# Bias seeds as four matmul passes on 32-row tiles, the three parts of the bias side by side in each row group

## The chip, the cores and the metric

The kernel runs on one core of a Trainium2 chip. The metric is the device time of one execution in microseconds (us), the median of the runs. Times inside an execution come from one profiled execution and count from the start of its span.

## The reference

Two layers, each with a residual and a layer norm, on x of 32 batches of 512 x 1024 f32. Layer 0 is a graph attention; layer 1 multiplies by W = adj * adj and adds a bias. It is this bias that the change is about.

```python
# layer 0: q, k = wq.x, wk.x over the 512 channels; scores = leaky_relu(q + k)
att = softmax(scores, axis=-1)
agg = einsum('bcn,bmn->bcm', x, att)
x = layernorm(x + relu(einsum('oc,bcm->bom', adj, agg) + bm[None, :, None]))
# layer 1
W = adj * adj
x = layernorm(x + einsum('bnf,nm->bmf', x, W) + bias)    # bias has 1024 elements
```

## The kernel before, in words

The work goes batch by batch, with four batches in flight. For each batch the kernel projects x (`project`, L320, into PSUM banks A, B and C), ranks the 1024 query values instead of forming the 1024 x 1024 softmax (`place` L390, `count` L417), scatters the projected rows by rank into a table in DRAM (`send` L403), reads the table back in blocks (`fetch` L445), forms prefix sums with nine small matmul steps (`table` L494, `table_out` L506, `carry` L515, `table_store` L521), gathers each row's sums from the table (`pick` L532), mixes them (`scale`, `gain`), turns the result (`turn` L584), adds the residual and normalises (`add`, `square`, `root0`, `finish` L614, which writes the four tiles of y at L619 on ScalarE), and then multiplies by W with a seven-product scheme (`multiply` L660) into PSUM banks A, B and C. `read` (L675) takes the products out, and `stats`, `root`, `shift`, `apply` and `store` finish the batch.

The order of all steps is written out by hand, as lists of step names: `BEGIN` (L844) for the start-up, `SLOT` (L910) once for each turn of the loop, 28 turns in all, and `END` (L874). Each engine takes its instructions in that order; SP issues the loads, table transfers and stores in that order too, and GpSimd (POOL) issues the indirect DMAs.

The bias enters through PSUM. `seed_bias` (steps sb0, sb1, sb2 in `BEGIN`) splits the f32 bias, broadcast over 128 partitions in y[:, 0], into three bf16 parts, one after the other: VectorE casts what is left of the bias into the bf16 view of y[:, 1] (L203, 128 x 1024), copies one row of it into `seeds` (L205), and subtracts the part from the bias (L209). Part i goes into partition 32 * i of a 128-row tile that is zero elsewhere. The first half of the 1024 columns is the bias of the left half, the second half the difference of right and left (L202). `seed` (L645, steps sA and sB) then begins the accumulation in banks A and B of each batch with two passes each: a matmul of an all-ones 128 x 128 stationary with the 128 x 512 rows of `seeds`, so that every output row receives the sum of the three parts. In `SLOT` the order on TensorE is t8 (table step, L501), sA, sB, then m0, m1, m3, m2, m6 and so on (L666); m6 is the first product that needs the last two tiles of y. In `BEGIN` sB and sA of batch 0 are apart, and in `END` the pairs are in part apart.

In `BEGIN` the steps around the bias are, in order: sb0, a few projections, fe (the fetch of batch 0), sb1, sb2, and then c0 (`count`, L419, on ScalarE). For the first two batches `count` and `place` write their unneeded output into y[:, 1] (`junk`, L277), which is the buffer that also holds the bf16 part of the bias.

Of the kernel before, what the change touches and what calls it, by code (L numbers as in the profile page):

```python
# [9 lines left out]
BF16 = mybir.dt.bfloat16  # L10
# [13 lines left out]
def gat_gcn_resnorm_kernel(  # L24
# [11 lines left out]
    nc = tc.nc  # L36
    P = 128
# [3 lines left out]
    H = 512  # L41
# [13 lines left out]
    const = ctx.enter_context(tc.tile_pool(name="const", bufs=1))  # L55
# [19 lines left out]
    for i, a in enumerate((wq, wk, bm)):  # L75
        nc.scalar.dma_start(
            out=vec[i * CT : (i + 1) * CT, :], in_=a.rearrange("(t p) -> t p", p=P)
        )
    nbm = const.tile([P, CT], F32, name="nbm")
    seeds = const.tile([P, 2, H], BF16, name="seeds")  # L80
    nc.vector.memset(seeds, 0.0)
    ones = const.tile([P, 1], BF16, name="ones")
    nc.vector.memset(ones, 1.0)
# [3 lines left out]
    for half in range(2):  # L87
        p0 = half * G
        nc.gpsimd.affine_select(
            out=tri[p0 : p0 + G, 0, :], in_=tri[p0 : p0 + G, 0, :], pattern=[[-2, G]],  # L90
# [3 lines left out]
            out=tri[p0 : p0 + G, 1, :], in_=tri[p0 : p0 + G, 1, :], pattern=[[2, G]],  # L94
# [3 lines left out]
    for row, i in ((0, 0), (G, 1)):  # L98
# [14 lines left out]
        out=first, in_=first, pattern=[[-1, 2 * N - P]], compare_op=ALU.is_ge,  # L113
# [28 lines left out]
    for td in tdb:  # L142
        nc.sync.dma_start(
            out=td.rearrange("(s u) c -> s u c", u=3)[N:NS, 0, :], in_=zs[P + N - NS : P, 0, 0:ZW]
        )
        odd = td.rearrange("(s w u) c -> s w (u c)", w=2, u=3)
        for r in range(0, NS // 2, P):
            n = min(P, NS // 2 - r)
            nc.sync.dma_start(
                out=odd[r : r + n, 0, ZW : 3 * ZW].rearrange("p (j c) -> p j c", j=2)[:, :, 0:1],  # L150
                in_=zs[0:n, 0:2, 1:2],
            )
            nc.sync.dma_start(
                out=odd[r : r + n, 1, ZW : 3 * ZW].rearrange("p (j c) -> p j c", j=2),
                in_=zs[0:n, 0:2, 0:ZW],
# [7 lines left out]
    def bank(tag, shape, name):  # L163
        return ps.tile(shape, F32, name=name, tag=tag)
# [32 lines left out]
    def seed_bias(b, i):  # L197

        part = yall[:, 1, 0:H].bitcast(BF16)
        b0 = yall[:, 0]  # L200
        if i == 0:
            nc.vector.tensor_tensor(b0[:, H:N], b0[:, H:N], b0[:, 0:H], ALU.subtract)  # L202
        nc.vector.tensor_copy(part, b0)  # L203
        row = 32 * i
        nc.vector.tensor_copy(  # L205
            seeds[row : row + 1].rearrange("p h c -> p (h c)"), part[row : row + 1]
        )
        if i < 2:
            nc.vector.tensor_tensor(b0, b0, part, ALU.subtract)  # L209

# [432 lines left out]
        nc.vector.tensor_tensor(part(b, name), part(b, of), part(b, by), ALU.subtract)  # L643

    def seed(b, at):  # L645

        o = ops[b, at] = bank(at, [P, 2, H], f"o{at}_{b}")
        for m in range(2):
            nc.tensor.matmul(
                o[:, m, :], ones.to_broadcast([P, P]), seeds[:, "AB".index(at), :],  # L650
                start=True, stop=True,
            )

    products = (
# [135 lines left out]
    for ot in range(CT):  # L790
# [10 lines left out]
        also(-1, f"av{ot}", apply, ot)  # L801
        also(-1, f"so{ot}", store, ot)
    also(0, "sA", seed, "A")
    also(0, "sB", seed, "B")
    for i in range(NM):
        also(0, f"m{i}", multiply, i)
# [12 lines left out]
    for i in range(3):  # L819
        also(0, f"sb{i}", seed_bias, i)  # L820
# [145 lines left out]
```

## Time and profile before

| | |
|---|---|
| median of three runs | 2203.01 us (2202.25 to 2207.36) |
| profiled execution, whole time | 2203.48 us |
| its span, first to last instruction | 2201.8 us |
| granted TensorE clock, mean | 0.989 |
| TensorE busy | 2109.1 us (96%) |
| VectorE busy | 1776.1 us (81%) |
| ScalarE busy | 1653.9 us (75%) |
| GpSimd busy | 986.5 us (45%) |
| bias passes (L649) | 128 in all, 376 to 392 ns each as recorded |
| copies into `seeds` (L205) | 3, median 418 ns |
| casts of the bias (L203) | 3, median 693 ns |

In the profile PE is TensorE's matmul, PEld its weight loads, DVE VectorE, ACT ScalarE, POOL GpSimd, and SPq the queue on which SP issues DMAs. L12 is line 12 of the kernel. A recorded matmul lasts until its result is through the array, so that matmuls that follow each other overlap in the records; the distance from one start to the next is what a pass costs. An f32 matmul shows as two records. A form such as 128*64 is the tile of the array that a matmul uses: 128 rows, 64 columns. A bracket at the end of a timeline line gives the idle time before it and what ended it.

### The profile page before, as it was taken

What the parts mean: (1) busy time and instruction counts of PE and PEld (TensorE: products, weight loads), DVE (VectorE), ACT (ScalarE), POOL (GpSimd) and SP (SyncE); (2) the same over time, 40 slices, a digit from 0 to 9 for tenths busy, and PEclk for the clock granted to TensorE, in tenths of its full rate; (3) what the DMA queues carried; (4) which work ended last, traced back from release to release, by engine and by line L of the source; (5) the groups of instructions that cost most, each with busy time, mean ns of one, the idle gap of its engine ahead of it and who ended that gap; (6) DMA issues with size and microseconds to landing.
All of it is one profiled execution on the core that took longest, in us unless ns stands there. A gap on an engine that the chain in (4) does not pass through costs nothing.

```text
span 2201.8 us, 35460 instructions
## 1 busy us (share of the span) xinstructions
PE 2109.1 (96%) x11697; PEld 1235.6 (56%) x11697; DVE 1776.1 (81%) x3576; ACT 1653.9 (75%) x2758; POOL 986.5 (45%) x1291
## 2 busy tenths in 40 slices
PE   7879999999999999999999999999999999999877
PEld 5446555566555566555566555556555556655433
DVE  7568888888888888888888888788888888888666
ACT  1577777887777887777887777888777788777765
POOL 1344455443455444445443445444445544445442
PEclk9989999999999999999999999999999999999998
DMA  7568888777888778888877889878888877888762
GB/s 249 162 224 255 263 272 280 260 236 244 263 257 280 251 240 256 262 260 280 259 244 239 270 255 282 264 244 245 263 256 279 278 247 238 260 264 270 220 206 96
DMA packets 178768, 548.84 MB, mean 249 GB/s; under 512 B 27020, under 2 KB 27032, under 8 KB 178584
## 3 DMA queue, kind: packets, MB, share of 16 engines
q1 hardware_dynamic: 121216, 277.05, 43.8%
q0 software_dynamic: 57344, 269.52, 34.4%
q8 instruction: 93, 1.52, 0.3%
q14 instruction: 91, 0.75, 0.1%
q10 hardware_dynamic: 24, 0.01, 0.0%
HBM read 338.17 MB, written 208.30 MB: 248 GB/s over the span
## 4 chain that ended last, share of the span: by engine, by line
PE 73%; ACT 8%; DMA 5%; issue 4%; DVE 4%; POOL 4%; SPq 1%; POOLq 0%; DVEq 0%; ACTq 0%
PE zp_A L329 17%; PE oA L666 15%; PE tp L501 12%; PE zp_B L329 7%; PE oB L666 7%; PE op L587 5%; PE zp_C L329 4%; PE oC L666 4%; DMA zs<-td 3%; ACT rows L573 1%; ACT y L619 1%; DMA td<-zrow,ranki 1%; ACT v L689 1%; POOL zs L519 1%; PE qb L367 1%
## 5 line engine op out<-in xcount | busy, mean ns | idle before, releaser
L578 DVE SCALAR_TENSOR_TENSOR rows<-rows,ra 128x512 f32<-128x512 f32 x512 | 365.7, 738 | 19.5 <-ACT rows L573 15.7
L501 PE MATMUL tp<-zs,lq 128*64 128x257 f32 x2304 | 338.3, 394 | 27.3 <-POOL zs L519 16.6
L406 POOL DMA_INDIRECT td<-zrow,ranki x256 | 268.3, 1048 | 213.7 <-DVE idx L430 80.2
L666 PE MATMUL oA<-y,adj_sb 128*128 128x512 f32 x768 | 352.2, 601 | 9.8 <-ACT y L619 5.9
L534 POOL DMA_INDIRECT rows<-td,idx x256 | 297.2, 1161 | 90.2 <-issue 68.7
L394 DVE SCALAR_TENSOR_TENSOR junk<-qb,zrow,first 128x1024 int8<-128x1024 f32 x240 | 307.0, 1279 | 10.9 <-PE qb L367 4.0
L519 POOL COPY zs<-ts 1x513 f32<-1x513 f32 x128 | 92.0, 719 | 477.9 <-ACT ts L513 477.7
L329 PE MATMUL zp_A<-wb,x 128*64 128x257 f32 (+1 forms) x1536 | 280.3, 388 | 13.9 <-ACT v L689 6.5
L419 ACT ACTIVATE junk<-lq,kc 128x1024 int8<-128x1024 f32 x240 | 274.5, 1144 | 2.0
L594 DVE SCALAR_TENSOR_TENSOR y<-op,nbm,x 128x1024 f32<-128x1024 f32 x128 | 163.8, 1282 | 128.8 <-PE op L587 128.6
L666 PEld LDWEIGHTS oA<-y,adj_sb 128*128 128x128 f32 x768 | 146.5, 192 | 189.0 <-issue 139.5
L501 PEld LDWEIGHTS tp<-zs,lq 128*64 128x64 f32 x2304 | 171.1, 137 | 135.1 <-POOL zs L519 37.0
L573 ACT ACTIVATE rows<-rows,ra 128x512 f32<-128x512 f32 x256 | 180.0, 718 | 80.0 <-DVE ra L566 78.4
L329 PEld LDWEIGHTS zp_A<-wb,x 128*64 128x64 f32 (+1 forms) x1536 | 178.6, 155 | 77.4 <-ACT v L689 17.8
L350 ACT COPY zrow<-zp_A 128x514 f32<-128x514 f32 x192 | 112.7, 587 | 143.6 <-PE zp_A L329 129.8
L519 POOL COPY zs<-zs 1x513 f32<-1x513 f32 x128 | 79.0, 617 | 253.3 <-ACT zs L513 253.3
L619 ACT ACTIVATE y<-y,nb,r 128x1024 f32<-128x1024 f32 x128 | 158.8, 1241 | 4.3
L695 DVE BATCH_NORM_STATS2 st<-v 128x6 f32<-128x512 f32 x240 | 151.8, 674 | 0.0
L603 ACT ACTIVATE x<-y,nm 128x1024 f32<-128x1024 f32 x128 | 147.2, 1150 | 4.2
L719 ACT ACTIVATE v<-v,nb,rs 128x1024 f32<-128x1024 f32 x120 | 148.1, 1234 | 2.3 <-DVE nb L711 1.4
L587 PE MATMUL op<-ident,rows 128*128 128x128 f32 x1024 | 141.5, 283 | 4.2 <-DVE rows L578 2.0
L587 PEld LDWEIGHTS op<-ident,rows 128*128 128x128 f32 x1024 | 114.9, 143 | 46.0 <-issue 24.6
(162 smaller groups left out, 3802.6 us busy)
## 6 DMA issues: line engine op xcount, KB each, us to landing
x<-in_x_dram SPq DMA_DIRECT2D x128, 512.0 KB, 4.5
out_dram<-v SPq DMA_DIRECT2D x120, 512.0 KB, 2.9
zs<-td SPq DMA_DIRECT2D x64, 602.3 KB, 9.5
td<-zs SPq DMA_DIRECT2D x288, 120.2 KB, 4.3
td<-ts SPq DMA_DIRECT2D x224, 120.2 KB, 2.0
zs<-td SPq DMA_DIRECT2D x64, 240.9 KB, 6.9
zs<-td SPq DMA_DIRECT2D x96, 120.5 KB, 7.2
td<-zs SPq DMA_DIRECT2D x8, 514.0 KB, 7.6
```

What stands on the lines that cost most here:

```text
L329: nc.tensor.matmul(zp[n : n + wide, m, 0:CE], side(b, g, a)[:, c, m * P + n : m * P + n + wide], wb[:, w, c, :], start=first and c == 0, s ...
L394: nc.vector.scalar_tensor_tensor(junk(b)[:, 0:N], qbs[b], zrow[:, nt, 0:1], first[:, o : o + N], ALU.subtract, ALU.is_lt, accum_out=rank[: ...
L406: sc = nc.gpsimd.indirect_dma_start(out=td[:, :], out_offset=bass.IndirectOffsetOnAxis(ap=ranki[:, nt : nt + 1], axis=0), in_=zrow[:, nt, ...
L419: nc.scalar.activation(junk(b)[:, N : 2 * N], qs[b], AF.Sign, bias=kcs[b][:, nt : nt + 1], accum_out=signs(b)[:, nt : nt + 1],)
L501: nc.tensor.matmul(tp[i * G : (i + 1) * G, h, 0:CE], lw[:, ks[i], :], zs[:, j, 1 + h * CE : 1 + (h + 1) * CE], start=True, stop=True,)
L519: copy(zs[row : row + 1, to, 1:ZW], ts[row : row + 1, 0 : ZW - 1])
L534: nc.gpsimd.indirect_dma_start(out=rows[:, mt, :], out_offset=None, in_=tdb[b % 2].rearrange("(s u) c -> s (u c)", u=3), in_offset=bass.In ...
L573: nc.scalar.activation(u, u, AF.Copy, scale=ratios(b)[:, k, 1:2])
L578: nc.vector.scalar_tensor_tensor(u, rg[:, k, i, 1 : C + 1], ratios(b)[:, k, i : i + 1], u, ALU.mult, ALU.add)
L587: nc.tensor.transpose(op[:, mt * P : (mt + 1) * P], rg[:, mt, 1, 1 + ot * P : 1 + (ot + 1) * P], ident)
L619: nc.scalar.activation(yall[:, ot], yall[:, ot], AF.Identity, bias=nb, scale=r)
L666: nc.tensor.matmul(o[:, m, :], quarters[w][:, a, m * P : (m + 1) * P], part(b, y)[:, a, :], start=fresh and a == 0, stop=a == CT // 2 - 1, ...
```

## The change

`seeds` becomes one tile of 128 partitions by 512 columns. The array's rows are taken as four groups of 32. Group g holds the three parts of one half of the bias in its partitions 32g, 32g + 1 and 32g + 2: the first half for g = 0 and 1, the second for g = 2 and 3. A pass contracts only these three rows, in the tile of 32 rows and 128 columns that its partitions name: groups 0 and 1 serve bank A, groups 2 and 3 bank B. Since part i now has to lie in partition 32g + i, the copy on VectorE is replaced by four small DMAs on SP for each part, from row i of the bf16 view to the four groups. The lists of steps are not touched; lines behind L205 move by one (the bias passes from L649 to L651).

```diff
-    seeds = const.tile([P, 2, H], BF16, name="seeds")
+    seeds = const.tile([P, H], BF16, name="seeds")
...
         nc.vector.tensor_copy(part, b0)
-        row = 32 * i
-        nc.vector.tensor_copy(
-            seeds[row : row + 1].rearrange("p h c -> p (h c)"), part[row : row + 1]
-        )
+        for g in range(4):
+            h = g // 2
+            nc.sync.dma_start(
+                out=seeds[32 * g + i : 32 * g + i + 1, :], in_=part[i : i + 1, h * H : (h + 1) * H]
+            )
         if i < 2:
             nc.vector.tensor_tensor(b0, b0, part, ALU.subtract)
...
     def seed(b, at):
-
         o = ops[b, at] = bank(at, [P, 2, H], f"o{at}_{b}")
         for m in range(2):
+            g = 2 * "AB".index(at) + m
+            of = slice(32 * g, 32 * g + 3)
             nc.tensor.matmul(
-                o[:, m, :], ones.to_broadcast([P, P]), seeds[:, "AB".index(at), :],
-                start=True, stop=True,
+                o[:, m, :], ones[of].to_broadcast([3, P]), seeds[of], start=True, stop=True
             )
```

## The prediction

> **What bounds the kernel now.** I read the page first, for the chain of waits that ended last, then the TensorE timeline around the bias passes of one turn of the loop (batch 14; the other 27 turns with all four passes together look alike), then the other engines there, and last the start-up, where the change adds transfers.
>
> The page's chain, shares of the span:
>
> ```profile
> PE 73%; ACT 8%; DMA 5%; issue 4%; DVE 4%; POOL 4%; SPq 1%; POOLq 0%; DVEq 0%; ACTq 0%
> ```
>
> TensorE carries the end. Followed piece by piece, this chain runs through the bias passes (L649) in 21 of those 28 turns. TensorE's timeline (start, length, engine, line, operands, form, count):
>
> ```profile
> 1008.61 1.24 PE L501 MATMUL tp<-zs,lq 128*64 128x257 f32 x8
> 1009.78 0.60 PE L649 MATMUL oA<-seeds,ones 128*128 128x512 bf16 x2
> 1010.22 0.59 PE L649 MATMUL oB<-seeds,ones 128*128 128x512 bf16 x2
> 1010.65 3.60 PE L666 MATMUL oA<-y,adj_sb 128*128 128x512 f32 x8
> ```
>
> Four passes start 0.226, 0.216 and 0.216 us apart, and the first product follows 0.216 us after the last: 0.874 us in all, back to back. That looks like time on the path. Eight microseconds later the product into oC (m6) needs the fourth tile of y. TensorE's weight loads, in a narrower window:
>
> ```profile
> 1018.29 0.30 PEld L666 LDWEIGHTS oC<-y,adj_sb 128*128 128x128 f32 x2 [0.57 <-ACT y L619]
> ```
>
> The load sat idle 0.57 us until ScalarE delivered y, then began at once. The timelines of ScalarE and of GpSimd:
>
> ```profile
> 1014.29 1.01 ACT L689 COPY v<-oA 128x1024 f32<-128x1024 f32 x1
> ...
> 1017.00 1.24 ACT L619 ACTIVATE y<-y,nb,r 128x1024 f32<-128x1024 f32 x1
> ```
>
> ```profile
> 1016.05 0.58 POOL L611 TENSOR_TENSOR r<-r,mhalf 128x1 f32<-128x1 f32 x1
> ```
>
> y ends at 1018.24; the matmul that needs it starts at 1018.38. ScalarE shows no idle row from 1002.75 to 1024.6, and the root that y needs ends on GpSimd at 1016.63, behind queued indirect DMAs. Neither hangs on the bias passes. So beside TensorE's path lies a second one that is only 0.10 us shorter (0.144 us between end and start, less the 0.044 us that such a handover takes at its shortest in this trace).
>
> The start-up, all engines:
>
> ```profile
> 61.99 3.61 SPq L457 DMA_DIRECT2D zs<-td  x6
> ...
> 63.26 0.69 DVE L203 CAST y<-y 128x1024 bf16<-128x1024 f32 x1
> ...
> 64.50 1.15 ACT L419 ACTIVATE y<-v,kc 128x1024 int8<-128x1024 f32 x1
> ...
> 66.49 0.59 ACT L350 COPY zrow<-zp_A 128x514 f32<-128x514 f32 x1 [0.74 <-PE zp_A L329]
> ...
> 74.56 0.69 ACT L467 ACTIVATE w<-zs,bw,el 128x7 f32<-128x7 f32 x2 [1.78 <-DMA zs<-td]
> ```
>
> and the chain of waits there (start, length, what):
>
> ```profile
> 65.15 9.32 DMA zs<-td
> 74.51 0.05 issue
> 74.56 0.41 ACT w L467
> 74.99 1.03 DVE lq L479 x2
> ```
>
> The big table fetch (L452, L457: eight transfers, issued 61.08 to 65.60, the last landing at 74.47) sets the start-up; ScalarE's L467 waits for it, and the ranking (L394) of batch 1 follows.
>
> **Part 1: four passes on row tiles.** The passes stay four, of 512 columns, into four different banks; each now contracts 3 rows on a 32-row tile. In the trace no matmul runs on row tiles. The nearest row is the column tiles (128*64): there two matmuls on different tiles start 7 to 8 ns apart and the pairs 0.21 us apart, so the two overlap. With starts 8 ns apart the pack takes 0.216 + 3 x 0.008 = 0.24 us. The Trainium skill (TensorE: Matmul & The Clock Gate, "Measured speedup vs the span model") gives 3.07 times for four row tiles of 512 columns: estimate 0.864 / 3.07 = 0.28 us. I take 0.28.
>
> Against this stands another rule of the skill (TensorEngine Tiling (Array Packing), "Key Properties"): a change of tiling mode drains TensorE. The row agrees and prices it: from 128*64 to 128*128 the first f32 matmul of 257 columns comes 0.308 us after the last, where 0.214 is its stream, and the second 0.321 after the first, where 0.217 is usual, as its weights could not be loaded ahead: 0.094 + 0.104 = 0.20 us. The entry (0.310 us from the table pass to the first bias pass) is a change of mode already and stays. The exit becomes a new one. New stretch 0.28 + 0.20 = 0.48 us, saved 0.39 us a turn. By the drain rule without overlap, the stretch would be 0.874 + 0.20: 0.20 lost. The ends are +0.20 and -0.43; I take -0.39, since the column-tile row does show overlap.
>
> On the path I count only 0.10 of it: after that the wait for y ends last, and the rest becomes a stall at m6. Five turns stall there already (0.6 to 1.9 us) and five stall later for weights from VectorE (L479, 0.4 to 1.9 us): no gain. 18 x 0.10 = **-1.8 us**. The other four batches have the pairs apart from each other; each pair saves about 0.2 and each added change of mode costs 0.1 to 0.2: 0, within 0.5 either way.
>
> **Part 2: twelve transfers for three copies.** Removed: three copies of 0.41 us on VectorE (L205); they lie in a stretch where VectorE waits for TensorE and ScalarE anyway, so 0, and the halved memset (0.485 us at the very start) 0 too. Added, on SP's queue: four small transfers after each of three casts. The instruction order of the changed kernel has SP as: four, the eight of the fetch, eight.
> - First part: cast over at 56.24; SP is idle until 61.08; four issues of 0.41 us, about 2 us to land (a 120 KB table store issued at 75.74, with nothing before it in the queue, took 1.93 us): done by 60, before the second cast (60.45 without its copy). Cost 0, and the fetch is not held.
> - Second part: cast over at 61.15, but its transfers stand behind the fetch and issue from 65.6 to 67.2. They land behind the fetch's data: a table store issued at 70.89 landed at 74.67, 3.8 us later. So about 74.7.
> - Third part: its cast overwrites the buffer that those transfers read, so VectorE, in order, waits from 62.4 to 74.7 (it ran at 63.26). Cast 0.69, four issues to 76.65 for the last, 2.0 to land: 78.65. Queued behind the waiting cast on VectorE are the adds into zrow (L348, 67.11) and the block weights (L479, 68.53), for which TensorE's table passes (L501) wait.
> - ScalarE's first count (L419, 64.50) writes its junk over the same buffer and waits until 78.65: 14.15 us late, and all of ScalarE behind it. Of its waits before 74.56, 0.74 (L350) and 1.78 (L467) are used up: 14.15 - 2.5 = **+11.6 us** where the chain passes at L467. Behind it I find no wait for anything that does not descend from this chain, so it carries to the first turn.
>
> Bounds. The Trainium skill (DMA: Bandwidth & Descriptors, "Queues, rings and completion order") says that completion is not first-in-first-out per issuing engine, so the second part might land early, near 69; the row of the store at 70.89 says otherwise. By the rule the sum changes little: the last seed transfer reuses the semaphore of the fetch's last, so it issues after 74.47 and lands at 76.5: +9.5. Upward, if a small transfer takes 4.9 us (the median of the 1 KB stores in the list of DMA issues): +14.5.
>
> **Sum.** 11.6 - 1.8 = +9.8 us. Against the profiled execution (span 2201.8, 1.7 around it, 2203.5) 2213.3; the median of the runs is 0.5 lower, so 2213.0 to the nearest half. My own range for this case is 2208 to 2217.
>
> **Rivals.** (a) *The whole saving counts*: y moves with the passes. For it: the chain of waits passes L649 in 21 of 28 turns. Against it: ScalarE without a gap and the 0.10 us. 28 x 0.39 = 10.9 against 11.6 gives 2204, no change; from 0.18 us a turn on the path it decides. (b) *No overlap*: rows tiled but streamed one by one. No row of the trace shows row tiles side by side. Then each turn loses 0.20, with TensorE on the path: 28 x 0.20 = 5.6, in all +17.2, 2220.5. (c) *The start-up is hidden*: the count does not wait, or the delay is made up before the first turn; 2203.5 - 1.8 = 2201.7. Against it, the order on SP and the 74.47.
>
> **How the numbers follow.** The forecast case 0.70, (a) 0.12, (b) 0.11, (c) 0.07. The range 2204 to 2221 leaves out (c) and the tails of (a) and (b). A measurement of this kernel tells about 0.3% (6.6 us) from no change: 2196.4 to 2209.6. Slower: nearly all of the forecast case and (b), 0.75; within: (a), most of (c), the low tail of the forecast case, 0.22; faster 0.03.
>
> **What would show it.** Third cast near 75 and the first count near 78 to 79 instead of 64.5; first bias pass of batch 1 (221.1) near 232.7; bias passes with starts under 0.05 us apart, and 0.45 to 0.5 us from the first to the first product; m6's second weight in a real stall of some 0.3 us behind y; the 28 turns together 1 to 3 us shorter. Wrong if the turns shrink by 0.3 us each, if the passes still start 0.21 apart, or if the first turn begins where it did.

## The result and the profile after

The changed kernel takes 2219.15 us, median of six runs (2216.49 to 2223.83), beside 2203.37 for the kernel before (six runs, 2199.94 to 2207.36): ratio 1.0072, 95% interval 1.0056 to 1.0088. The forecast was 2213.0, in a range of 2204 to 2221; the prediction's narrower range for its own case was 2208 to 2217. The profiled execution took 2218.85 us, span 2217.1, against 2203.48 and 2201.8: +15.4 where the sum had +9.8.

The page's chain of waits, shares of the span by engine:

```profile
PE 60%; ACT 11%; DVE 10%; DMA 7%; issue 7%; POOL 3%; SPq 1%; DVEq 0%; POOLq 0%; ACTq 0%
```

Less of the end now hangs on TensorE (73% before), more on ScalarE and VectorE. Two places changed: the start-up and each turn. The start-up first, all engines of the changed kernel (start, length, engine, line, operands, form, count; in brackets the idle time before it and what ended it):

```profile
55.68 2.52 SPq L206 DMA_DIRECT2D seeds<-y  x4
...
60.67 3.58 SPq L458 DMA_DIRECT2D zs<-td  x6
...
64.34 12.40 SPq L206 DMA_DIRECT2D seeds<-y  x8
...
73.63 0.69 DVE L203 CAST y<-y 128x1024 bf16<-128x1024 f32 x1 [11.38 <-DMA seeds<-y]
78.04 1.15 ACT L420 ACTIVATE y<-v,kc 128x1024 int8<-128x1024 f32 x1 [14.23 <-DMA seeds<-y]
...
79.81 3.52 PE L330 MATMUL zp_A<-wb,v 128*64 128x257 f32 x16 [13.04 <-ACT zrow L351]
...
86.65 0.67 ACT L468 ACTIVATE w<-zs,bw,el 128x7 f32<-128x7 f32 x2
```

The third cast stood idle for 11.38 us and the first count for 14.23, both until a transfer into `seeds` had landed. The fetch itself was not held: its issues start at 59.88 here, at 61.08 before. ScalarE's second set of block weights (L468, L467 before) comes at 86.65 instead of 74.56. The chain of waits through the same stretch (start, length, what):

```profile
66.88 6.63 DMA seeds<-y
...
73.63 0.70 DVE y L203
...
76.16 1.65 DMA seeds<-y
...
79.81 3.52 PE zp_A L330 x16
```

The second part's last transfer lands 6.6 us after its issue, behind the fetch; the third part's, with an empty queue, 1.7 us after. The last line was not foreseen: 16 projection passes in 3.52 us. In the kernel before, 16 passes of this form take 1.95:

```profile
67.14 1.95 PE L329 MATMUL zp_A<-wb,v 128*64 128x257 f32 x16
```

The table of stretches says why, here a row of the kernel before and below it rows of the changed kernel (stretch, its length, the busy time of TensorE, its weight loads, VectorE, ScalarE and GpSimd, the granted TensorE clock, DMA share, GB/s):

```profile
67.00:68.00 1.00, 1.00 (x12) 0.63 (x10) 0.69 (x1) 1.00 (x2) 0.00 (x0) 1.00 0.85 257
```

```profile
80.00:81.00 1.00, 1.00 (x6) 0.57 (x6) 0.48 (x1) 1.00 (x3) 0.00 (x0) 0.50 0.00 0
81.00:82.00 1.00, 1.00 (x6) 0.47 (x4) 0.79 (x3) 0.45 (x2) 0.00 (x0) 0.50 0.00 0
...
83.00:84.00 1.00, 1.00 (x12) 0.50 (x8) 0.63 (x2) 0.59 (x1) 0.00 (x0) 0.99 0.00 0
```

After 13 us without work TensorE was granted half its clock, and got the whole back 3.2 us after it resumed. The kernel before shows 1.00 there. So the wait cost 1.57 us on top of its length, for a slow restart.

Now a typical turn of the loop, with its bias passes at 1152.90. TensorE:

```profile
1152.90 0.39 PE L651 MATMUL oA<-seeds,ones 3*128 3x512 bf16 x2
1152.90 0.39 PE L651 MATMUL oB<-seeds,ones 3*128 3x512 bf16 x2
1153.22 3.70 PE L667 MATMUL oA<-y,adj_sb 128*128 128x512 f32 x8
```

The load at m6 that needs the fourth tile of y, from the timeline of the weight loads:

```profile
1161.32 0.30 PEld L667 LDWEIGHTS oC<-y,adj_sb 128*128 128x128 f32 x2 [0.94 <-ACT y L620]
```

And ScalarE, which delivers that tile:

```profile
1157.35 0.99 ACT L690 COPY v<-oA 128x1024 f32<-128x1024 f32 x1
...
1160.03 1.24 ACT L620 ACTIVATE y<-y,nb,r 128x1024 f32<-128x1024 f32 x1
```

The four passes do run side by side: their starts are 3 to 4 ns apart, and the first product follows 0.324 us after the first pass instead of 0.874. Its second pass then comes after 0.533 us instead of 0.429, since its weights were not loaded ahead. m6 begins 0.446 us earlier than before (7.296 us after the first bias pass, 7.742 before), and then stands: y ends at 1161.27, the load that needs it has been idle for 0.94 us, where it was 0.57.

| profiled executions, us | before | after | difference |
|---|---|---|---|
| first cast of the bias | 55.55 | 54.96 | -0.59 |
| first count (L419, L420) | 64.50 | 78.04 | +13.54 |
| second block weights (L467, L468) | 74.56 | 86.65 | +12.09 |
| first bias pass (batch 0) | 149.25 | 161.16 | +11.9 |
| first turn's bias passes | 221.12 | 234.70 | +13.58 |
| 28 turns | 1833.89 | 1833.43 | -0.46 |
| from there to the end | 146.8 | 149.0 | +2.2 |

### The profile page after: what moved, and what is told of

It reads as the page before. It is cut to its first block, busy times and chain, and to the rows that moved or that the text cites. A ratio compares the mean times of both kernels' runs of the same rounds, so it can differ in the third digit from the quotient of the medians.

```text
span 2217.1 us, 35475 instructions
## 1 busy us (share of the span) xinstructions
PE 2107.0 (95%) x11697; PEld 1235.1 (56%) x11697; DVE 1779.8 (80%) x3573; ACT 1654.1 (75%) x2758; POOL 984.4 (44%) x1291
## 4 chain that ended last, share of the span: by engine, by line
PE 60%; ACT 11%; DVE 10%; DMA 7%; issue 7%; POOL 3%; SPq 1%; DVEq 0%; POOLq 0%; ACTq 0%
PE zp_A L330 17%; PE tp L502 11%; PE oA L667 9%; PE zp_B L330 8%; PE op L588 5%; DVE junk L395 4%; PE zp_C L330 4%; DMA zs<-td 4%; ACT y L620 3%; PE oB L667 3%; PE oC L667 2%; DMA td<-zrow,ranki 2%; ACT v L690 1%; ACT rows L574 1%; PE qb L368 1%
## 5 line engine op out<-in xcount | busy, mean ns | idle before, releaser
L502 PE MATMUL tp<-zs,lq 128*64 128x257 f32 x2304 | 343.0, 395 | 29.1 <-POOL zs L520 15.7
L420 ACT ACTIVATE junk<-lq,kc 128x1024 int8<-128x1024 f32 x240 | 274.4, 1143 | 2.0
```

The costliest lines, as they stand in the source:

```text
L420: nc.scalar.activation(junk(b)[:, N : 2 * N], qs[b], AF.Sign, bias=kcs[b][:, nt : nt + 1], accum_out=signs(b)[:, nt : nt + 1],)
L502: nc.tensor.matmul(tp[i * G : (i + 1) * G, h, 0:CE], lw[:, ks[i], :], zs[:, j, 1 + h * CE : 1 + (h + 1) * CE], start=True, stop=True,)
```

## The experiments

The theory after the result: the two waits for the `seeds` transfers carry the whole loss, the passes give about nothing because y comes last, and they would give over 0.4 us a turn if it did not. The rivals: SP's queue itself is the cost (twelve issues, and the fetch beside them); or the row tiles are, by their change of mode.

**e1_own_buffers.** The parts are cast into three spare buffers, so that no engine waits for a transfer; all twelve remain.

```diff
-        part = yall[:, 1, 0:H].bitcast(BF16)
+        part = rows[:, i, 0:H].bitcast(BF16)
```

> The changed kernel, but each bf16 part of the bias is cast into its own buffer (a part of the tile rows that nothing uses in the start-up) instead of the shared y[:, 1]. The twelve transfers stay where they are on SP, and the passes stay on row tiles; only the two waits (third cast on VectorE for the second part's transfers, first count on ScalarE for the third part's) have no cause any more. My theory: the third cast comes at about 62.5 and the first count at about 64.5 us again, and the whole start-up delay of 11.9 us (first bias pass 161.2 against 149.3) goes: time near 2203. If the queue on SP itself is the cause (table stores behind eight more transfers), the first bias pass stays near 161 and the time near 2218. If the passes on row tiles bring the other 3 to 4 us of the loss, it stays near 2206 to 2207.

Measured: 2202.39 us, median of 14 runs, beside 2202.63 for the kernel before on the same chip; ratio 0.9998 (0.9987 to 1.0009). The start-up of this kernel:

```profile
62.91 0.69 DVE L203 CAST rows<-y 128x1024 bf16<-128x1024 f32 x1
...
64.32 1.15 ACT L420 ACTIVATE y<-v,kc 128x1024 int8<-128x1024 f32 x1
...
64.78 8.96 SPq L206 DMA_DIRECT2D seeds<-rows  x8
```

The cast and the count are back where they were, the eight transfers still follow the fetch and land as late as they like. The interval is 2 to 3 us wide on either side, and within it nothing is left for the queue: the two waits are the loss, and one line of code takes them away.

**e2_transfers_only.** The 128-row passes of before, with the twelve transfers; two of each four go to `spare` (the name stands here for a part of the tile `rows` that nobody reads there), the other two where the copy had put the row.

```diff
-        nc.vector.tensor_copy(
-            seeds[row : row + 1].rearrange("p h c -> p (h c)"), part[row : row + 1]
-        )
+        for g in range(4):
+            h = g // 2
+            to = seeds if g % 2 == 0 else spare
+            nc.sync.dma_start(
+                out=to[32 * i : 32 * i + 1, h, :], in_=part[i : i + 1, h * H : (h + 1) * H]
+            )
```

> The kernel before with its four passes on 128 rows, but the copies into the bias rows are made by four transfers on SP for each part (two of the four go to a place that nothing reads), with the shared buffer. So the start-up of the change alone. My theory: the same two waits, first bias pass near 161, turns as before: 2203.4 + 12 to 14 = 2215 to 2217. Rival, that the row-tiled passes slow the kernel: about 2204.

Measured: 2216.58 us, median of six, ratio 1.0059 (1.0037 to 1.0080). The same wait, without any row tile:

```profile
74.19 0.69 DVE L203 CAST y<-y 128x1024 bf16<-128x1024 f32 x1 [11.67 <-DMA rows<-y]
```

This profiled execution, the slowest of the six at 2224.88 us, also has a longer slow restart than the changed kernel. The row at which TensorE resumes, and two of its table of stretches:

```profile
80.37 3.70 PE L331 MATMUL zp_A<-wb,v 128*64 128x257 f32 x16 [13.34 <-ACT zrow L352]
```

```profile
85.00:86.00 1.00, 1.00 (x8) 0.48 (x5) 1.00 (x2) 0.17 (x1) 0.00 (x0) 0.50 0.00 0
86.00:87.00 1.00, 1.00 (x12) 0.65 (x10) 0.01 (x1) 0.97 (x2) 0.52 (x1) 0.88 0.00 0
```

The granted clock is 0.50 until about 86.2, 5.9 us after TensorE resumed, where it was 3.2 us in the changed kernel.

**e3_passes_only.** The row-tile passes without a transfer: VectorE places the parts with a mask of one column per part, two instructions each. These six take 0.76 us each and stand ahead of the first count, which waits for them until 65.8. Of the edit, the part that replaces the transfers:

```diff
...
+        for h in range(2):
+            ps_ = slice(64 * h, 64 * h + 64)
+            nc.vector.scalar_tensor_tensor(
+                seeds[ps_], part[ps_, h * H : (h + 1) * H], mask[ps_, i : i + 1], seeds[ps_],
+                ALU.mult, ALU.add,
+            )
...
```

> The row-tiled passes of the change alone: the parts are put side by side into each row group by VectorE (for each part two masked multiply-adds of 64 x 512 in place of the copy), so there are no transfers and no waits for them; 1 to 2 us more work on VectorE in the start-up, where it idles. My theory: the stretch from the first pass to the first product is 0.324 us as in the changed kernel instead of 0.874, and its weights cost 0.10 more behind it, but only 0.1 us or less a turn counts, since the product m6 then waits for the fourth tile of y: 2200 to 2203. Rival, that all of it counts: 28 x 0.45 = 12.6 us less, about 2191. Rival, that the added changes of tiling mode cost in the end (the 2.2 us that the changed kernel loses behind the 28 turns): about 2205.

Measured: 2202.1 us, median of 14, ratio 0.9998 (0.9986 to 1.0011). The 28 turns take 1833.06 us. The passes alone are worth nothing here that this interval, 3 us on either side, would show; the whole saving (rival a, some 2191) is refuted, and so is a loss of 5.6 us by passes that do not overlap (rival b). e1, which has these passes and all twelve transfers, differs from it by 0.3 us: the second sign that the queue is not the cost.

**e4_one_group.** As e3, but all four passes use the same group of rows, so that they can't lie side by side. Of the edit against e3, the passes (`seeds` also has its two halves again, and the parts lie in its rows 0 to 2):

```diff
-            g = 2 * "AB".index(at) + m
-            of = slice(32 * g, 32 * g + 3)
...
-                o[:, m, :], ones[of].to_broadcast([3, P]), seeds[of], start=True, stop=True
+                o[:, m, :], ones[0:3].to_broadcast([3, P]), seeds[0:3, "AB".index(at)],
+                start=True, stop=True,
```

> As the run with the passes alone, but all four passes use the same row group (rows 0 to 2), so that they are on row tiles, with the change of mode behind them, and cannot overlap. My theory: passes 0.216 apart, then 0.31 to the first product and 0.10 for its weights: 0.20 more a turn than before, all of it on TensorE's path: 28 x 0.20 = 5.6, about 2208 to 2209. If passes in one row group overlap after all: as the run before. If TensorE has slack there: about 2203.

Measured: 2208.41 us, median of 22, ratio 1.0027 (1.0017 to 1.0037). TensorE:

```profile
1007.32 0.60 PE L652 MATMUL oA<-seeds,ones 3*128 3x512 bf16 x2
1007.76 0.59 PE L652 MATMUL oB<-seeds,ones 3*128 3x512 bf16 x2
1008.28 3.70 PE L669 MATMUL oA<-y,adj_sb 128*128 128x512 f32 x8
```

The passes start 0.22 us apart again, and the first product comes 0.96 us after the first pass. The typical turn is 65.20 us against 65.01: the change of mode costs 0.2 us, fully on TensorE's path. This is rival b, built. Its price was right in the typical turn and in the medians (+5.8 us for 28 x 0.20 = 5.6); the profiled execution, one of the two fastest, has +3.05 in its 28 turns. Of the layouts run here, the one on different groups of rows avoids it.

**e6_early_y_before and e5_early_y_passes.** If y is what swallows the passes' gain, an earlier y must free it. Only the order of a turn is edited, the same way in both: the count c0 goes behind the last tile of y on ScalarE (it stood ahead of `read`'s copy of oA), and the root rt3 ahead of the gathers pi3 on GpSimd. e6 does it to the kernel before, as a control; e5 to e3.

```diff
-    ... T1 m1 c0 sd1 r2 m3 rdp1 pi3 r3 y2 m2 rt3 r4 pi2 y3 m6 ...
+    ... T1 m1 sd1 r2 m3 rdp1 rt3 pi3 r3 y2 m2 r4 pi2 y3 c0 m6 ...
```

> The kernel before with only the order of a turn changed: step c0 (the count into y[:,1], ScalarE) goes behind y3, and rt3 (the root that y3 needs, GpSimd) goes ahead of pi3 (the gathers it was queued behind), so that the fourth tile of y is ready about 1 us earlier. It is the control for the next kernel. If TensorE's own passes carry a typical turn (my theory: y ended 0.10 us before it would hold m6), an earlier y brings nothing by itself in the typical turn, only in the five turns in which m6 stalled for y (0.4 to 1.6 us each, some of which the later count may give back elsewhere): 2196 to 2204, most likely 2202. If y carried the turns already, 28 x 0.4 us less or more: 2192 or below.

> The same order of a turn (count behind y3, root ahead of the gathers) together with the row-tile passes without the transfers (the kernel whose passes alone measured 2202.1). Theory: the passes free 0.446 us a turn on TensorE, of which the fourth tile of y lets through only 0.075, because the product that waits for it stalls 0.27 us and then loads its next weights in the open for 0.10 us. With y earlier neither is left: each turn is shorter than in the control by about 0.44 us, up to 28 x 0.44 = 12 us, less the turns that wait for something later: 7 to 12 us below the control, about 2191 to 2196. Rival 1, that something other than y caps the turns (VectorE's block weights or ScalarE as a whole): within 3 us of the control, about 2200 to 2202. Rival 2, that the freed time was not real: equal to the control within 1 us.

Measured on one chip, beside 2203.02 for the kernel before: e6 2198.94 us (22 runs), ratio 0.9976 (0.9965 to 0.9986); e5 2190.52 (five runs), ratio 0.9941 (0.9926 to 0.9957), at the low end of what was expected. The same passes that were worth nothing in the old order are worth 8.4 us in the new one. ScalarE of e5 in a typical turn, whose first bias pass is at 1193.93:

```profile
1197.99 1.01 ACT L693 COPY v<-oA 128x1024 f32<-128x1024 f32 x1 [0.79 <-PE oA L670]
...
1200.69 1.24 ACT L623 ACTIVATE y<-y,nb,r 128x1024 f32<-128x1024 f32 x1
```

The weight loads of m6 in the same turn:

```profile
1201.22 0.19 PEld L670 LDWEIGHTS oC<-y,adj_sb 128*128 128x128 f32 x1 [0.24 <-issue]
1201.98 0.30 PEld L670 LDWEIGHTS oC<-y,adj_sb 128*128 128x128 f32 x2 [0.56 <-ACT y L623]
1202.52 0.19 PEld L670 LDWEIGHTS oC<-y,adj_sb 128*128 128x128 f32 x1 [0.24 <-issue]
```

ScalarE now waits for oA instead of running without a gap, so y moves with TensorE: it ends 8.00 us after the first bias pass, where it was 8.37 in the changed kernel. The load of m6 is idle 0.56 us as in the kernel before, and in all 28 turns m6's passes are 0.43 us apart. The smallest turns are 64.6 us against 65.0 in e6, as the theory has it; all 28 take 1817.66 us against 1827.32, 0.345 a turn, since some turns wait for something else. Rivals 1 and 2 of e5 fall. The control's own gain of 4 us lay in its range, but past the value held most likely (2202): the five turns that had stalled for y are gone, and their time did not come back elsewhere.

**e7_count_waits and e8_cast_waits.** Each leaves one of the two waits in the changed kernel. e7, on the cast:

```diff
-        part = yall[:, 1, 0:H].bitcast(BF16)
+        part = (yall[:, 1, 0:H] if i < 2 else rows[:, 2, 0:H]).bitcast(BF16)
```

e8, on the count:

```diff
-            junk(b)[:, N : 2 * N], qs[b], AF.Sign, ...
+            rows[:, 7, 0:H].bitcast(I8)[:, 0:N] if b == 0 else junk(b)[:, N : 2 * N], qs[b], AF.Sign, ...
```

> The changed kernel with the third part in a buffer of its own: VectorE's third cast waits for nothing, but ScalarE's first count still writes over the buffer of the first two parts and so waits for the second part's transfers, which landed at 73.6 us. Theory: the count starts near 73.6 to 74 instead of 64.3 (9.3 late instead of 13.6), of which 3 us are made up as in the changed kernel: +6.3, and +1.5 more if TensorE, idle for some 8 us, comes back at half clock as it did after 13 us: about 2208.5 to 2211 against 2202.4 with both waits gone. If the third part's own landing was what mattered (the cast and the transfers behind it), no loss: 2202 to 2203. If the wait's length hardly matters, as in the changed kernel: 2217 to 2219.

> The changed kernel with the other wait alone: the counts of the first batch write their unneeded output elsewhere, so ScalarE does not wait, and VectorE's third cast still waits for the second part's transfers (73.6 us). Queued behind it on VectorE are the add into zrow (67.1 in the kernel before, now near 74.4) and the block weights (68.5). Theory: both are 7 us late, TensorE waits with its table passes, and 1 to 2 us of it are made up in the wait for the fetch: +5 to +6 us and up to 1.5 more for a TensorE clock halved by idling, 2207.5 to 2210. If only ScalarE's wait carries the loss: 2202 to 2203.

Measured beside 2200.63 for the kernel before: e7 2212.24 us (six runs), ratio 1.0054 (1.0039 to 1.0069); e8 2210.93 (six runs), ratio 1.0043 (1.0029 to 1.0056). Either wait alone costs most of what both do, since each of the two ends here with the second part's landing. The start-up of e7, where only ScalarE waits:

```profile
72.62 1.15 ACT L420 ACTIVATE y<-v,kc 128x1024 int8<-128x1024 f32 x1 [10.48 <-DMA seeds<-y]
...
74.39 3.40 PE L330 MATMUL zp_A<-wb,v 128*64 128x257 f32 x16 [9.29 <-ACT zrow L351]
```

And of e8, where only VectorE waits:

```profile
72.19 0.69 DVE L203 CAST y<-y 128x1024 bf16<-128x1024 f32 x1 [11.26 <-DMA seeds<-y]
...
73.74 2.17 PE L502 MATMUL tp<-zs,lq 128*64 128x257 f32 x8 [6.78 <-DVE lq L480]
```

In both, TensorE runs dry for 7 to 9 us and comes back at a granted clock of 0.50. It has 1.00 back 3.0 us later in e7 and 3.7 in e8, within these stretches (e7, then e8):

```profile
77.00:78.00 1.00, 1.00 (x10) 0.66 (x8) 0.15 (x1) 0.15 (x1) 0.00 (x0) 0.82 0.00 0
```

```profile
77.00:78.00 1.00, 1.00 (x10) 1.00 (x8) 0.00 (x0) 0.97 (x2) 0.20 (x1) 0.77 0.43 125
```

From each execution's own first cast to its first bias pass it is 8.3 us longer than before in e7 and 4.7 in e8, 12.5 in the changed kernel. By the ratios the losses are 11.9 and 9.5 us, some 4 to 5 us more than the traces' start-ups and 2 to 3 us above the upper ends expected. That difference is not explained. The profiled execution of e7 is the fastest of its six (2206.95), and a slow restart as long as that of e2 would account for 1.1 to 1.5 us of it (half of the longer time at half clock).

**e9_own_buffers_early_y.** The change with both repairs, the edits shown for e1 and e5.

> The change with its transfers, the parts in buffers of their own (both waits gone), and the order of a turn that delivers y earlier. If the start-up waits and the late y are all that kept the change from paying, this gives what the passes without transfers gave in that order (2190.5): 2189 to 2193, 0.5 to 0.6% faster than the kernel before. If the transfers on SP cost anything by themselves, 2194 or more.

Measured: 2188.07 us (six runs, 2184.2 to 2191.28) beside 2200.63; ratio 0.9936 (0.9921 to 0.9950). With e5 it is the fastest here; it keeps the change's transfers and passes as they are.

## Why the prediction was right, step by step

The direction and both places were right, and the time lay in the range, 6 us above the forecast. It lay above the prediction's own range for its case, though (2208 to 2217); the wider one reached up to it because it left room for rival (b), which the passes refute. So the cause was foreseen, and that the number fell in the range is in part luck. The steps:

- *The second part's transfers land behind the fetch, near 74.7; the cast waits.* Right: 73.63. The rule of the Trainium skill that completion is not first-in-first-out (DMA: Bandwidth & Descriptors, "Queues, rings and completion order") allowed it to land near 69; in all four kernels that wait for it, cast or count start between 72.2 and 74.2, after the fetch.
- *The count is 14.15 us late.* Right: 13.54, or 14.13 counted from the execution's own first cast, which was 0.59 early.
- *Of that 2.5 is absorbed, +11.6 at the second block weights.* Nearly: +12.1, or 12.7 by the execution's own start. A term was missing, the halved clock (+1.57); what is left for the waits used up is then 14.13 + 1.57 - 12.7 = 3.0, for 2.5. e1 shows that the start-up's loss goes with the waits, e2 that it comes without row tiles.
- *The pass stretch 0.874 becomes 0.48, saving 0.39.* Right in mechanism; the new stretch is 0.428 (0.324 to the first product and 0.104 behind it), the saving 0.446. The prediction's estimate of 0.28 for the pack was too dear: with the exit's drain of 0.094 taken off, 0.23 is left, what the column-tile row of before gave (0.24). e4 shows the rest: on one group of rows nothing overlaps, and the exit costs 0.20.
- *Only 0.10 a turn counts, as y comes next.* This term was mis-sized. m6's stall is real (0.27 us, 0.3 was named), but behind the stall the next weights are loaded in the open too: the step behind it takes 0.533 us instead of 0.432. So 0.446 - 0.27 - 0.10 = 0.075 us is left in a typical turn, and the 28 turns shrank by 0.46, not by 1.8 (by 1.6 in e1, 0.8 in e3). e5 against e6 confirms it by taking the stall away: -0.345 a turn.
- *Rivals.* (a), the whole saving, is refuted by e3 in this order of steps; with y moved most of it came (8.4 us, e5 against e6). (b), no overlap, is refuted by the starts 3 to 4 ns apart; e4 is what it would have cost (the prediction's own terms add up to 2220.7 for it, not 2220.5). (c), a hidden start-up, is refuted by e2.

The profiled execution's excess over the sum, 15.4 - 9.8 = 5.6, is: +0.9 at the first bias pass by its own start (12.5 for 11.6), +1.7 between there and the first turn, +1.35 in the turns, +2.2 at the end, -0.6 for the early start. The second is one wait, ScalarE for the fetch of the next batch's table:

```profile
213.50 0.69 ACT L468 ACTIVATE w<-zs,bw,el 128x7 f32<-128x7 f32 x2 [1.69 <-DMA zs<-td]
```

It isn't the change's: that stretch is 73.0 us in e3, which adds no transfer, and 71.8 in e1, which has all of them, against 73.55 after and 71.87 before. The stretch behind the turns, too, is 149.1 us in e1 and in e6 and 146.6 in e7. Single executions differ by 2 us in each; the medians (e1 equal to before) hold no such loss. By the ratios the loss is 15.9 us with the passes (12.3 to 19.4) and 13.0 without them, in e2 (8.2 to 17.6), which these runs do not tell apart.

## What to carry to other kernels

A copy that becomes a DMA holds its source until it lands: look for who overwrites the source next, on every engine, and for what is ahead in that queue. A few bytes behind a bulk fetch are as late as the fetch, and a second buffer (one line) can be the whole difference. And when a stage gets faster without the end moving, find the operand that is now late and move its producer: of the two edits of e5 the passes alone gave nothing and the order alone 4 us, together they gave 12.5.

## What the runs showed of the hardware

- Matmuls of 3 rows and 512 columns on four different groups of 32 rows start 3 to 4 ns apart and take 0.23 us together (0.324 us to the first product, less the 0.094 of the exit), where one takes 0.216; on one group they start 0.22 us apart.
- Leaving the row tiles for f32 products on the whole array costs 0.2 us: 0.09 until the first product and 0.10 for weights that are not loaded ahead. A stall of m6 on its weights costs that second 0.10 again (0.533 us for the next step instead of 0.43).
- TensorE that idled for 7 to 13 us resumed at a granted clock of 0.50. It had 1.00 back 3.2 us later in the changed kernel, 3.0 in e7, 3.7 in e8 and 5.9 in e2. The Trainium skill (TensorE: Matmul & The Clock Gate, "What's actually happening") asks for at least one busy window of about 3.4 us, which is near the first three; why e2 took longer is not shown. The slow restart cost 1.57 us on top of the wait in the changed kernel; for e2 it is some 2.9 by estimate, half of the 5.9 us at half clock.
- A 1 KB transfer took 1.7 us from issue to landing with nothing ahead in its queue, and 6.6 us behind a table fetch of eight transfers.
